# Cross attention: scores by quarters of the keys with VectorE's transposes, and the query folding in pieces

## The chip, the cores and the metric

The kernel runs on one core of a Trainium2 chip. The core has five engines with queues of their own: TensorE (PE in the profile; its weight loads are PEld), VectorE (DVE), ScalarE (ACT), GpSimd (POOL) and SyncE (SP). They share the on-chip memory SBUF. TensorE writes to PSUM, eight banks of 2 KB in each of 128 partitions, and VectorE and ScalarE read it. The metric is the device time of one execution in microseconds.

## The reference, cut to what matters

The network has four layers of cross attention, token mixing and a feed-forward part, twelve blocks in all. `x` is 16 batches of 64 tokens by 256, `ctx` 16 batches of 1024 keys by 192, all in float32. The change touches the cross attention of the first three layers:

```python
x = x + L0_xattn(layernorm(x), ctx, Wq, Wk, Wv, Wo)
...
x = x + L1_xattn(layernorm(x), ctx, Wq, Wk, Wv, Wo, bo)
...
x = x + L2_xattn(layernorm(x), ctx, Wq, Wk, Wv, Wo, bo)

def xattn(q_tokens, kv_tokens, Wq, Wk, Wv, Wo):   # per batch and head
    q, k, v = q_tokens @ Wq, kv_tokens @ Wk, kv_tokens @ Wv
    attn = softmax(q @ k.T * scale)
    return concat_heads(attn @ v) @ Wo            # + bo in L1 and L2
```

L0 has 16 heads of 16, L1 and L2 have 8 heads of 64.

## The kernel before, in words

The three blocks are two functions: `xattn_direct` for L0 and `xattn_folded` for L1 and L2. Both write their instructions in an order by hand: `set_order(True)` chains what goes to PE (`mm`, `tr`, lines 188 and 191), and the queues `dve` and `act` (line 72) do the same for VectorE and ScalarE. So each of these engines works strictly in the order of the program text, and an instruction that waits holds up all behind it. GpSimd's instructions are not chained by hand; they follow the program's order. Waits between engines come from the tiles that instructions read and write. A tile pool with `bufs=n` gives n buffers in turn, and the next user of a buffer waits for the last reader.

**`xattn_direct`.** 64 steps, for 16 batches b and 4 groups c of four heads. `qb` holds the scaled queries, for each group with the rows of the two heads of a pair masked (`own`), so that one matmul gives scores of two heads. A step works one ahead:

- `scores(b, c)` of the next step: four matmuls, each with 32 rows of keys, 128 query columns and 512 keys, into two `pss` tiles of 1024 columns (pool `ps_s`, two buffers of two banks);
- `least`: VectorE's negated maximum over the 1024 keys of each tile;
- `transposes`: the last step's probabilities `pr` are turned in eight 128x128 blocks by PE into a `pst` bank and copied to `pT` by ScalarE and VectorE, half of them early in the step, half late;
- `exps`: ScalarE's exponential with its sum `sm`, one instruction a tile; `shares`: VectorE divides by the sum;
- `project(b + 1, c)`: a quarter of the next batch's keys and values into two `psp` banks, copied to `kT` or `v` by VectorE and ScalarE;
- `values`: 32 matmuls of `v` with `pT` into `o`, one half of the bank `both` for even and one for odd batches; `keep` copies it out once a batch, and `output(t)` multiplies by `Wo` and adds to the residual `X`.

`queries` makes `qb`: the two instructions that mask it read the same bank `psq`, one on VectorE and one on ScalarE.

**`xattn_folded`.** Queries are multiplied by the key weights first (`queries`, then `fold`, for each of four head pairs m into `qw`), so that scores are taken against the raw context. `folded(g)` does all four m for four batches, and runs whole at the start and before batches 4, 8 and 12. There are 32 steps, for batch b and half h of the heads, again with scores one step ahead:

- `scores`: `qw` against `cT`, by quarters `qa` of the keys (32 output partitions each), into four `pss` banks of a pool of five. The tensors are so laid out that the 32 queries of a quarter lie beside the keys, and `turn` can transpose `pr` in 32x32 blocks on VectorE (`dve.transpose`, STREAM_TRANSPOSE) instead of on PE;
- `least`: maxima of each bank, then minima over the four partition quarters by small VectorE instructions (`nw`, `nmm`); `exps`: eight exponentials of 256 columns; `sums`: a matmul with `same` adds the sums of the quarters; `shares` divides, half on ScalarE, half on VectorE;
- `values(b - 1, h)` and, where h is 1, `others(b - 1)` and `keep(b - 1)`: the context weighed by the probabilities;
- `output(g2)`, every fourth batch in the step with h = 0: multiply by `Wv` per head (`oc` to `oT`), then by `Wo`, and add to `X`.

The layer norm in front of it, `norm_T`, handles all eight token tiles before the first fold. In L1 the steps 3 to 11 also issue `conv_taps`, and 14 to 29 `tap_rows`, for the next block.

Of the kernel before, what the change touches and what calls it, by code (L numbers as in the profile page):

```python
# [15 lines left out]
P = 128  # L16
# [62 lines left out]
class Net:  # L79
# [200 lines left out]
    def xattn_direct(self, L):  # L280
# [7 lines left out]

        nc, tc, a = self.nc, self.tc, self.a
# [6 lines left out]
        with ExitStack() as es:  # L296
# [3 lines left out]
            ps_s = es.enter_context(tc.tile_pool(name=f"{L}ps_s", bufs=2, space=PSUM))  # L300
# [7 lines left out]
            nc.vector.tensor_scalar(own, own, 0.25, None, ALU.mult)  # L308
            vs = [one.tile([P, NKC, H, 32], F32, name=f"v{i}") for i in range(2)]
# [43 lines left out]
            ctxs, kTs, os_ = {}, {}, {}  # L353
            both = ps_o.tile([P, 2, 4, TQ], F32, name="o")

            def project(b, piece):
# [6 lines left out]
                if piece < 2:  # L363
# [11 lines left out]
                    for i, copy in enumerate((dve.tensor_copy, act.copy)):  # L375
                        copy(kTs[b][:, 2 * piece + i, :], ps[i])
                else:
# [17 lines left out]
                    for n, copy in enumerate((dve.tensor_copy, act.copy)):  # L395
                        j = 4 * n + 2 * jh
                        copy(v[:, j : j + 2, :, :16], ps[n].rearrange("p (i h d) -> p i h d", i=2, d=16))

            def scores(b, c):
                pss = [ps_s.tile([P, S], F32, tag="s", name="pss") for _ in range(2)]  # L400
                for n in range(2):
                    for e in range(2):
                        r = (n ^ (c % 2)) * 64 + e * 32
                        ql = qb[r : r + 32, c, b].rearrange("p h q -> p (h q)")
                        self.mm(pss[e][:, n * 512 : (n + 1) * 512], ql, kTs[b][r : r + 32, c, :])
                return pss

            def least(ps):
                nm = self.small.tile([P, 1], F32, tag="nm", name="nm", bufs=4)
                dve.tensor_reduce(nm, ps, AX.X, ALU.max, negate=True)  # L410
                return nm

            def exps(ps, nm):
                pr = thr.tile([P, S], F32, tag="pr", name="pr", bufs=4)
                sm = self.small.tile([P, 1], F32, tag="sm", name="sm", bufs=4)
                act.activation(pr, ps, AF.Exp, bias=nm, accum_out=sm)
                return pr, sm

            def shares(pr, sm):
                dve.reciprocal(sm, sm)  # L420
                dve.tensor_scalar(pr, pr, sm, None, ALU.mult)

            def transposes(dst, pr, jh, copy):
                pt = ps_t.tile([P, 512], F32, tag="t", name="pst")
                for j in range(4):
                    jj = jh * 4 + j
                    self.tr(pt[:, j * P : (j + 1) * P], pr[:, jj * P : (jj + 1) * P])
                copy(dst[:, jh * 4 : jh * 4 + 4, :], pt.rearrange("p (j q) -> p j q", q=P))

            def values(b, c, pT):  # L430
                o = both[:, b % 2]
                for j in range(NKC):
                    for h in range(4):
                        self.mm(
                            o[32 * h : 32 * h + 32, c, :],
                            vs[b % 2][:, j, 4 * c + h, :],
                            pT[:, j, h // 2, (h % 2) * TQ : (h % 2 + 1) * TQ],
                            j == 0,
                            j == NKC - 1,
                        )  # L440

            def keep(b):
                if b % 2 == 0:
                    os_[b // 2] = two.tile([P, 4, 2, TQ], F32, tag="oT", name="oT")
                act.copy(os_[b // 2][:, :, b % 2, :], both[:, b % 2])
# [14 lines left out]
            project(0, 0)  # L460
            project(0, 1)
# [3 lines left out]
            pss = scores(0, 0)  # L465
            prs = [exps(pss[e], least(pss[e])) for e in range(2)]
            project(0, 2)
            project(0, 3)
            for p in prs:
                shares(*p)  # L470
            last = None
            for i, (b, c) in enumerate(steps):
                ahead = steps[i + 1] if i + 1 < len(steps) else None
                nxt, nms = [None, None], [None, None]
                if ahead:
                    pss = scores(*ahead)
                    nms = [least(ps) for ps in pss]
                pT = thr.tile([P, NKC, 2, P], F32, tag="pT", name="pT")
                transposes(pT[:, :, 0, :], prs[0][0], 0, act.copy)
                transposes(pT[:, :, 0, :], prs[0][0], 1, dve.tensor_copy)  # L480
                if ahead:
                    nxt = [exps(pss[e], nms[e]) for e in range(2)]
                    shares(*nxt[0])
                if b + 1 < B:
                    project(b + 1, c)
                if last:
                    values(*last)
                if ahead:
                    shares(*nxt[1])
                transposes(pT[:, :, 1, :], prs[1][0], 0, dve.tensor_copy)  # L490
                transposes(pT[:, :, 1, :], prs[1][0], 1, act.copy)
# [6 lines left out]
                if c == 0 and last:  # L498
                    keep(b - 1)
                if c == 1 and b % 2 == 0 and b > 0:  # L500
                    output(b // 2 - 1)
                prs, last = nxt, (b, c, pT)
            values(*last)
            keep(B - 1)
# [3 lines left out]
    def xattn_folded(self, L):  # L508
# [18 lines left out]
        with ExitStack() as es:  # L527
# [9 lines left out]
            self.norm_T(ps_s, "s")  # L537
# [2140 lines left out]
```

## Time and profile before

| | |
|---|---|
| median of 3 runs | 3169.97 us (3168.56 to 3195.57) |
| the profiled execution | 3170.8 us, of which its span is 3168.8 us |
| PE, DVE, ACT, POOL busy | 2940.9, 1960.3, 1348.4, 712.7 us |
| scores of L0, first and last start | 30.9 and 494.4 us |
| scores of L1 | from 766.8 us |
| scores of L2 | from 1659.2 us |

A row of the profile's groups names the source line, engine and operation, the tiles written and read (`pss<-kT,qb`), their shapes, how often, the busy time and the mean duration in ns; the idle time in front of it and what ended it stand last. In the order of time a row gives start and duration in us, and in brackets the idle time of the engine before it with what released it. Most PE and VectorE instructions of the ordered parts carry line 188, 191 or 72, those of the helpers, so they are told apart by their tiles. A float32 matmul is two MATMUL rows. PEclk is the clock that TensorE was granted, 1.00 at full speed. Matmul durations overlap, so starts are the better measure.

### The profile page before, as it was taken

The numbers are of one execution on the slowest core, as the hardware profiler recorded it, in microseconds if no ns is written. First come the engines' busy times: TensorE is split into PE (matmuls) and PEld (weight loads), VectorE is DVE, ScalarE is ACT, GpSimd is POOL, SyncE is SP. The second block draws the span as 40 slices with busy tenths as digits, with TensorE's granted clock in tenths as the row PEclk, the third lists the DMA queues.
The fourth block names the chain that finished last, engine by engine and source line by source line (L and its number), as shares of the span: only waits on it lengthen the run. The fifth ranks groups of instructions, "written<-read, shape, count | busy, mean of one in ns | idle before, by whom it ended". The sixth has DMA issues, their size and how long they took to land.

```text
span 3168.8 us, 64106 instructions
## 1 busy us (share of the span) xinstructions
PE 2940.9 (93%) x26912; PEld 1772.9 (56%) x26912; DVE 1960.3 (62%) x4061; ACT 1348.4 (43%) x3035; POOL 712.7 (22%) x784
## 2 busy tenths in 40 slices
PE   7999999898899999979978999997999899998797
PEld 4666666665445544458854545434665455556676
DVE  6888886524666665971127676757884676765611
ACT  3555554312554541013324454438861255654211
POOL 1000002411110001014411000024771355541131
PEclk9999999999999999978988999998999999999889
DMA  2000000013223313017851222201111211210233
GB/s 74 32 32 32 28 22 15 14 37 105 61 78 92 98 45 82 21 65 270 294 162 53 70 71 73 59 21 39 41 54 37 64 57 63 70 44 14 94 108 122
DMA packets 73793, 223.00 MB, mean 70 GB/s; under 512 B 17457, under 2 KB 28580, under 8 KB 66594
## 3 DMA queue, kind: packets, MB, share of 16 engines
q1 hardware_dynamic: 45936, 113.99, 11.9%
q0 software_dynamic: 21840, 99.39, 9.4%
q10 hardware_dynamic: 5730, 5.53, 0.6%
q8 instruction: 212, 3.47, 0.5%
q14 instruction: 75, 0.61, 0.1%
HBM read 210.00 MB, written 12.66 MB: 70 GB/s over the span
## 4 chain that ended last, share of the span: by engine, by line
PE 79%; DVE 9%; issue 4%; ACT 4%; POOL 3%; DMA 1%; SPq 0%; ACTq 0%; POOLq 0%; DVEq 0%
PE pss L188 13%; PE o L188 12%; PE pu L188 6%; PE psp L188 5%; PE pkv L188 5%; PE pd L188 5%; PE py L188 4%; PE pst L191 4%; PE psc L188 3%; PE po L188 2%; DVE nm L72 2%; ACT pr L72 2%; PE pb L191 2%; PE psi L188 1%; PE psq L188 1%
## 5 line engine op out<-in xcount | busy, mean ns | idle before, releaser
L188 PE MATMUL pss<-cT,qw 128*32 128x256 f32 x8192 | 371.5, 387 | 23.0 <-ACT pr L72 23.0
L72 DVE TENSOR_REDUCE nm<-pss 128x2 f32<-128x512 f32 (+1 forms) x384 | 309.3, 861 | 86.3 <-PE pss L188 86.3
L188 PE MATMUL o<-pT,cx 128*64 128x512 f32 (+1 forms) x1024 | 355.4, 607 | 0.0
L72 ACT ACTIVATE pr<-pss,nmm 128x256 f32<-128x256 f32 x512 | 234.3, 483 | 164.8 <-DVE nmm L72 164.8
L188 PEld LDWEIGHTS pss<-cT,qw 128*32 128x32 f32 x8192 | 205.0, 110 | 173.0 <-ACT pr L72 33.1
L188 PEld LDWEIGHTS o<-pT,cx 128*64 128x64 f32 (+1 forms) x1024 | 127.8, 165 | 200.2 <-issue 187.8
L205 POOL TENSOR_SCALAR rs<-mv 128x8 f32<-128x8 f32 (+3 forms) x52 | 10.0, 193 | 877.1 <-DVE mv L221 444.4
L188 PE MATMUL pkv<-wx,cT 128*128 128x512 f32 (+1 forms) x512 | 193.3, 632 | 0.6 <-issue 0.6
L72 ACT ACTIVATE pr<-pr,sm 128x256 f32<-128x256 f32 x256 | 109.1, 497 | 184.2 <-DVE sm L72 184.2
L72 DVE TENSOR_SCALAR pr<-pr,sm 128x256 f32<-128x256 f32 (+1 forms) x384 | 170.6, 486 | 6.6
L72 DVE TENSOR_TENSOR_SCAN h<-dA,pb 128x512 f32<-128x512 f32 x128 | 154.5, 1217 | 15.8 <-PE pb L191 9.4
L1444 POOL TENSOR_TENSOR h<-h,cb 128x1024 f32<-128x1024 f32 x64 | 151.4, 2368 | 53.3 <-DVE h L72 51.0
L2304 DVE TENSOR_SCALAR y<-pd,row 128x256 f32<-128x256 f32 x39 | 18.9, 484 | 225.1 <-PE pd L188 175.7
L72 DVE STREAM_TRANSPOSE pT<-pr 128x1024 f32<-128x1024 f32 x128 | 151.8, 1224 | 2.2
L188 PE MATMUL pd<-wd,hT 128*128 128x256 f32 x656 | 149.3, 382 | 3.0 <-DVE hT L2492 1.4
L72 ACT ACTIVATE pr<-pss,nm 128x1024 f32<-128x1024 f32 x128 | 142.5, 1113 | 11.4 <-DVE nm L72 8.8
L191 PE MATMUL pst<-ident,pr 128*128 128x128 f32 x1024 | 140.6, 280 | 5.8 <-DVE sm L72 1.9
L72 ACT COPY pT<-pst 128x512 f32<-128x512 f32 x128 | 74.9, 585 | 163.8 <-PE pst L191 163.8
L191 PEld LDWEIGHTS pst<-ident,pr 128*128 128x128 f32 x1024 | 109.4, 141 | 61.5 <-ACT pT L72 26.5
L188 PEld LDWEIGHTS pd<-wd,hT 128*128 128x128 f32 x656 | 123.1, 190 | 31.4 <-DVE hT L2492 6.2
L1618 POOL TENSOR_TENSOR rnk<-rnk,mhalf 128x8 f32<-128x8 f32 (+1 forms) x84 | 130.0, 1548 | 7.0
L188 PE MATMUL py<-h,ident 128*128 128x512 f32 x256 | 130.7, 596 | 0.0
(525 smaller groups left out, 5700.2 us busy)
## 6 DMA issues: line engine op xcount, KB each, us to landing
cT<-in_ctxT SPq DMA_DIRECT2D x32, 768.0 KB, 4.4
cx<-in_ctxP SPq DMA_DIRECT2D x32, 768.0 KB, 4.3
cT<-in_ctxT SPq DMA_DIRECT2D x32, 512.0 KB, 4.3
cT<-in_ctxT SPq DMA_DIRECT2D x64, 256.0 KB, 6.1
offb<-d_off SPq DMA_DIRECT2D x16, 576.0 KB, 3.6
cb<-d_C SPq DMA_DIRECT2D x16, 512.0 KB, 3.8
wu<-in_L_ffn_w POOLq DMA_DIRECT2D x8, 1024.0 KB
wd<-in_L_ffn_w POOLq DMA_DIRECT2D x8, 1024.0 KB
```

Source lines behind the costliest of these rows:

```text
L72: ins = getattr(self.engine, op)(*args, **kwargs)
L188: self.in_order(self.nc.tensor.matmul(out, lhsT=lhsT, rhs=rhs, start=start, stop=stop))
L191: self.in_order(self.nc.tensor.transpose(out, in_, self.ident))
L205: nc.gpsimd.tensor_scalar(t[:p, :n], in_, scale, eps, ALU.mult, ALU.add)
L1444: nc.gpsimd.tensor_tensor(hs[i], hs[i], cbs[hf, g], ALU.mult)
L1618: nc.gpsimd.tensor_tensor(r, r, self.mhalf[:, : n * H], ALU.pow)
L2304: nc.vector.tensor_scalar(y[:, i, :], po[:, i * D : (i + 1) * D], weight[:, g + i : g + i + 1], None, ALU.mult)
```

## The change

In `xattn_direct`, scores are taken for one half `hh` of a step at a time: 32 matmuls of 32 rows of keys by 32 query columns by 128 keys, by quarters `qa` of the keys. Both halves live in one tile `pss` of four banks with one buffer. `turn` on VectorE replaces `transposes` on PE. The maxima of the four quarters are gathered by four small GpSimd copies, reduced by VectorE, and spread by two more copies. Probabilities are no longer divided; the sums are added by PE once a batch (`sums`), spread over the partitions (`spread`) and multiplied into the values in `keep`. Both projection copies of a step go to ScalarE.

In `xattn_folded`, the norm works by halves of the tokens, `queries` and `fold` are issued one m at a time over the steps (`pieces`), `qw` is split in two tiles a group with three buffers, `output` is split into `heads` and `output(t)` in two steps, and the last batch's values are taken by halves of the columns.

```diff
-            ps_s = ... (name=f"{L}ps_s", bufs=2, space=PSUM)
+            ps_s = ... (name=f"{L}ps_s", bufs=1, space=PSUM)
...
+            pss = ps_s.tile([P, 2, 4, 2, P], F32, name="pss")
             both = ps_o.tile([P, 2, 4, TQ], F32, name="o")
...
+            def scores(b, c, hh):
+                kT = kTs[b][:, c].rearrange("p (k a y) -> p k a y", a=4, y=32)
+                for u in range(2):
+                    for qa in range(4):
+                        for n in range(2):
+                            for e in range(2):
+                                r = (n ^ (c % 2)) * 64 + e * 32
+                                self.mm(
+                                    pss[qa * 32 : (qa + 1) * 32, n, 2 * e + u, hh, :],
+                                    qb[r : r + 32, c, b, hh, u * 32 : (u + 1) * 32],
+                                    kT[r : r + 32, :, qa, :],
+                                )
+            def largest(hh):
+                nm = self.small.tile([P, 4], F32, tag="nm", name="nm", bufs=4)
+                dve.tensor_reduce(nm, pss[:, :, :, hh, :].rearrange("p n q k -> p q n k"), AX.XY, ALU.max, negate=True)
+                w = self.small.tile([32, 4, 4], F32, tag="nw", name="nw", bufs=4)
+                for qa in range(4):
+                    nc.gpsimd.tensor_copy(w[:, qa], nm[qa * 32 : (qa + 1) * 32])
+                return w
+            def least(w):
+                m = self.small.tile([P, 4], F32, tag="nmm", name="nmm", bufs=4)
+                dve.tensor_reduce(m[:32], w.rearrange("p a q -> p q a"), AX.X, ALU.min)
+                nc.gpsimd.tensor_copy(m[32:64], m[:32])
+                nc.gpsimd.tensor_copy(m[64:], m[:64])
+                return m
+            def exps(b, c, hh, m):
...
+                pr = thr.tile([P, 4, 2, P], F32, tag="pr", name="pr", bufs=3)
+                for q in range(4):
+                    act.activation(pr[:, q], pss[:, :, q, hh, :], AF.Exp, bias=m[:, q : q + 1],
+                        accum_out=sms[b][:, c, hh, q : q + 1])
+                return pr
+            def turn(b, c, hh, pr, lo=0, hi=4):
...
+                dve.transpose(
+                    pTs[b, c][:, :, hh, lo:hi].rearrange("p k q x -> p q k x"),
+                    pr[:, lo:hi].rearrange("p q n (k y) -> p q (n k) y", y=32),
+                )
+            def sums(b):
+                ps = both[:, 1].rearrange("p c q -> p (c q)")[:, :32]
+                for qa in range(4):
+                    self.mm(ps[qa * 32 : (qa + 1) * 32], same, sms[b].rearrange("p c h q -> p (c h q)"))
+                rc = two.tile([P, 32], F32, tag="rc", name="rc")
+                dve.reciprocal(rc, ps)
+                rds[b] = two.tile([P, 4, 2, 2, 2 * 32], F32, tag="rd", name="rd", bufs=1)
+                nc.gpsimd.tensor_tensor(
+                    rds[b].rearrange("p c h e (u x) -> p (c h e u) x", x=32), bc(rc, 2, 32), bc(same, 1, 32), ALU.mult
+                )
+            def spread(b):
+                for h in range(4):
+                    self.mm(both[32 * h : 32 * h + 32, 1], fourth, rds[b][:, :, h % 2, h // 2, :])
+                ra = two.tile([P, 4, TQ], F32, tag="ra", name="ra", bufs=1)
+                act.copy(ra, both[:, 1])
+                return ra
+            def keep(b, ra):
...
+                dve.tensor_tensor(os_[b // 2][:, :, b % 2, :], both[:, 0], ra, ALU.mult)
...
             for i, (b, c) in enumerate(steps):
                 ahead = steps[i + 1] if i + 1 < len(steps) else None
...
+                    scores(*ahead, 0)
+                    w = largest(0)
+                turn(b, c, 1, prs[1])
                 if ahead:
+                    prs[0] = exps(*ahead, 0, least(w))
                 if b + 1 < B:
+                    late = project(b + 1, c)
+                    act.copy(*late[0])
+                if ahead:
+                    scores(*ahead, 1)
+                    w = largest(1)
+                if c == 3:
+                    sums(b)
+                if c == 0 and last:
+                    ra = spread(b - 1)
                 if last:
                     values(*last)
                 if ahead:
+                    turn(*ahead, 0, prs[0], 0, 2)
+                    prs[1] = exps(*ahead, 1, least(w))
+                    turn(*ahead, 0, prs[0], 2, 4)
+                if c == 0 and last:
+                    keep(b - 1, ra)
+                if b + 1 < B:
+                    act.copy(*late[1])
```

In `xattn_folded`, cut to the order of the work:

```diff
-            self.norm_T(ps_s, "s")
...
             def queries(g, m):
-                ps = bank("psq")
+                ps = ps_t.tile([P, 512], F32, tag="t", name="psq")
...
             def fold(g, m):
-                if m == 0:
-                    qws[g] = two.tile([P, 2, G, H, TQ], F32, tag="qw", name="qw", bufs=1)
+                if m % 2 == 0:
+                    qws[g, m // 2] = two.tile([P, 2, G, 4, TQ], F32, tag="qw", name="qw", bufs=3)
-                pss = [bank("psqw") for _ in range(2)]
+                pss = [bank("psqw"), ps_t.tile([P, 512], F32, tag="t", name="psqw")]
...
-            folded(0)
+            norm(0)
+            normed(0)
+            for m in range(2):
+                queries(0, m)
+                fold(0, m)
             steps = [(b, h) for b in range(B) for h in range(2)]
             pss = scores(0, 0, None)
             now = exps(pss, least(pss))
+            for m in range(2, 4):
+                queries(0, m)
+                fold(0, m)
+            pieces = {8 * g + at: (g + 1, m) for g in range(B // G - 1) for m, at in enumerate((2, 4, 6, 7))}
+            pieces.update({0: (1, 0), 1: (1, 1)})
+            del pieces[2], pieces[4]
             for i, (b, h) in enumerate(steps):
-                if ahead and ahead[0] % G == 0 and ahead[1] == 0:
-                    folded(ahead[0] // G)
+                piece = pieces.get(i)
...
                 if ahead:
                     pss = scores(*ahead, lambda: sums(st, sm))
                 else:
+                    values(b - 1, range(4, NKC))
                     sums(st, sm)
                 dve.reciprocal(sm, st["sum"][:, :8])
                 shares(prs, sm, 1)
+                if piece:
+                    queries(*piece)
                 if ahead:
                     now = exps(pss, least(pss))
...
-                if b > 0:
-                    values(b - 1, h)
-                    if h == 1:
-                        others(b - 1)
-                        keep(b - 1)
+                if ahead and b > 0:
+                    values(b - 1, range(4 * h, 4 * h + 4))
+                if piece:
+                    fold(*piece)
+                if b > 0 and h == 1:
+                    others(b - 1)
+                    keep(b - 1)
+                if i == 1:
+                    norm(1)
+                if i == 2:
+                    normed(1)
...
-                if h == 0 and b % G2 == 1 and b > 1:
-                    output(b // G2 - 1)
+                if b % G2 == 1 and b > 1:
+                    if h == 0:
+                        heads(b // G2 - 1)
+                    else:
+                        for tt in range(T2 // P):
+                            output((b // G2 - 1) * T2 // P + tt)
...
-            for r in range(2):
-                values(B - 1, r)
-            others(B - 1)
+            for cols in (slice(0, 256), slice(256, 512)):
+                values(B - 1, range(NKC), cols)
+                others(B - 1, cols)
             keep(B - 1)
-            output(B // G2 - 1)
+            heads(B // G2 - 1)
+            for t in range(NT - T2 // P, NT):
+                output(t)
```

## The prediction

> **What bounds the kernel now.** I read the page, then busy time by stretches, then instructions in order of time in each stage that the change touches.
>
> ```profile
> PE 2940.9 (93%) x26912; PEld 1772.9 (56%) x26912; DVE 1960.3 (62%) x4061; ACT 1348.4 (43%) x3035; POOL 712.7 (22%) x784
> ```
>
> TensorE is the bound overall; whether it is in the touched stages shows in the stretches (the last three columns are granted clock, DMA share, GB/s):
>
> ```profile
> 31.00:477.00 446.00, 440.30 (x6208) 272.46 (x6208) 373.17 (x584) 251.37 (x438) 5.03 (x8) 1.00 0.09 30
> 778.00:799.00 21.00, 15.00 (x280) 8.06 (x274) 12.46 (x33) 11.09 (x42) 0.00 (x0) 0.83 0.22 52
> ```
>
> The first row is the steps of the first cross attention: PE busy 440.3 of 446 us, full clock. One of its 64 steps in order of time:
>
> ```profile
> 155.77 1.14 PE L188 MATMUL pss<-kT,qb 32*128 32x512 f32 x8
> 156.84 1.09 PE L191 MATMUL pst<-ident,pr 128*128 128x128 f32 x8
> 156.96 2.36 DVE L72 TENSOR_REDUCE nm<-pss 128x1 f32<-128x1024 f32 x2 [0.83 <-PE pss L188]
> 157.77 2.96 PE L188 MATMUL psp<-wv,cT 128*128 128x256 f32 x16
> 160.66 1.10 PE L188 MATMUL o<-pT,v 128*32 128x64 f32 x64
> 161.69 1.09 PE L191 MATMUL pst<-ident,pr 128*128 128x128 f32 x8
> 162.71 1.14 PE L188 MATMUL pss<-kT,qb 32*128 32x512 f32 x8
> ```
>
> PE starts: scores 1.07, transposes 0.93, projection 2.89, values 1.03, transposes 1.02: 6.94 us a step and no gap. With `output` and `queries`, which PE does between steps, the 63 steps from the first scores (30.9) to the last (494.4) take 463.5. VectorE works 6.2 us of it, ScalarE 4.6, hidden.
>
> **First cross attention, the good part.** Both sets of transposes leave PE: -1.95 us. Scores become 64 instructions a half, each 32 rows by 32 columns by 128 keys (a float32 matmul is two instructions). Nearest rows: `o` above, 64 instructions on four column tiles in 1.03 us, 16 ns each[...]; and, with eight tiles,
>
> ```profile
> 905.90 1.96 PE L188 MATMUL pss<-cT,qw 64*32 64x256 f32 x64
> 907.79 3.70 PE L188 MATMUL o<-pT,cx 128*128 128x512 f32 x8
> ```
>
> 64 in 1.88 us. The Trainium skill (TensorEngine Tiling (Array Packing), Theoretical Speedup) promises up to 16 times for 32x32 tiles. With 16 tiles and half the columns the 1.88 would be a quarter, 0.47 us. The 16 ns of `o` say 1.03, since each instruction has its weight load. Ends 0.47 and 1.88; I take 1.05, by `o`. PE then works 2 x 1.05 + 2.89 + 1.03 = 6.0 us a step, 0.9 less. VectorE loses the shares and pT copies and gains transposes at 1.2 us a half; ScalarE stays under 5 us. By busy time the step would be 6.0.
>
> **What it waits for.** `pss` is now one tile [P, 2, 4, 2, P] of four 2 KB banks, and the half `hh` is the second innermost axis: each bank holds keys of both halves. Both halves' scores, maxima and exponentials therefore use the same four banks. Two pairs of rows, each one DVE and one ACT instruction on disjoint interleaved outputs:
>
> ```profile
> 25.86 0.75 DVE L72 TENSOR_SCALAR qb<-psq,own 128x512 f32<-128x512 f32 x1 [1.19 <-PE psq L188]
> 26.64 0.69 ACT L72 ACTIVATE qb<-psq,own 128x512 f32<-128x512 f32 x1 [2.02 <-DVE qb L72]
> ...
> 761.80 0.69 DVE L72 COPY qw<-psqw 128x512 f32<-128x512 f32 x1 [3.58 <-PE psqw L188]
> 761.84 0.58 ACT L72 COPY qw<-psqw 128x512 f32<-128x512 f32 x1 [0.94 <-PE psqw L188]
> ```
>
> The `qw` pair reads two banks and runs side by side. The `qb` pair reads one bank and runs one after the other, 26.61 to 26.64, in all eight cases. Interleaved SBUF output isn't the reason (`qw` has it too); the shared bank is. That row shows two readers of the same columns. The rule of the skill (PSUM — Partial Sum Buffer, PSUM bank collisions raise a hardware error) goes further: any two of TensorE, VectorE and ScalarE must be kept apart per bank and quadrant, writes too, disjoint columns too. If only overlapping columns counted, half 1's scores could run under half 0's exponentials; by the rule they wait for the last of them. I take the rule, since the row has its sign.
>
> Then the program's order is one chain: scores 0, maxima 0, exponentials 0, scores 1, maxima 1, exponentials 1, next step. Its links, per half:
> - scores 1.05, hop 0.1 (hops of 0.03 to 0.1 are read between rows);
> - `largest`: 1024 elements from PSUM, 1.22 as `nm` now;
> - four GpSimd copies 32x4. No such row exists; nearest is
>
> ```profile
> L790 POOL COPY after<-gts 64x64 f32<-64x64 f32 x2 | 0.5, 234 | 0.0
> ```
>
> and TENSOR_SCALAR 128x4 at 192 ns. I take 0.18 each, with the hop 0.80; ends 0.1 each (a GpSimd memset of 32x1 is 91 ns) and 0.5 (moving between quadrants is unseen);
> - VectorE's 16-element minimum 0.19 and two hops 0.07, then two dependent GpSimd copies with hops 0.54;
> - four exponentials of 256 with accumulators. Existing ones
>
> ```profile
> L72 ACT ACTIVATE pr<-pss,nmm 128x256 f32<-128x256 f32 x512 | 234.3, 483 | 164.8 <-DVE nmm L72 164.8
> ```
>
> start 0.45 us apart, four take 1.92 to the last accumulator read; hops 0.13.
>
> Half 1 is 1.05 + 0.1 + 1.22 + 0.80 + 0.19 + 0.07 + 0.54 + 1.92 + 0.13 = 6.0. In half 0 the 1.2 us transpose of the previous half stands ahead of the minimum in VectorE's queue and outlasts the 0.80 of copies: 6.4. Step 12.4. The projection (2.9) lies beside half 0's chain, values (1.0) beside half 1's: hidden, so PE's savings buy nothing. Moving projection copies to ScalarE, `keep`, `output`, `queries`: in PE's or ScalarE's idle time, nothing.
>
> Two extras. `sums` puts on GpSimd, once a batch, a 1024-element product `rds`, between half 1's copies and its last two copies; its nearest row, a TENSOR_TENSOR 128x1024, is 2.37 us, about 2.1 of it in the chain: 16 x 2.1 = 34 us, 0.5 a step (ends 0 and 0.6). `rc`, `spread` and `ra` share the bank of `both` with values, which has slack. And PE idles some 2.4 us in half 0 and 3.9 in half 1. The second stretch above has idle gaps of 3.0 us every 10.4 us, and a mean clock of 0.83. For scores that follow them I add 0.5 a step (ends 0 and 1.5).
>
> Sum: 13.4 us a step, 63 steps: 844 against 463.5, **+381 us**. The ends of the unknown prices: all low, 11.1 us a step (+236); all high, about 17 (+608).
>
> **Second and third attention.** Steps there are PE-bound too: 9.15 and 12.74 us alternating, without gaps. Folding by pieces moves PE work of 2.1 us a piece and removes waits such as
>
> ```profile
> 859.81 2.08 PE L188 MATMUL psqw<-qT,wkT 64*128 64x256 f32 x8 [4.57 <-ACT qT L72]
> ...
> 1753.52 1.13 PE L188 MATMUL psqw<-qT,wkT 64*128 64x256 f32 x8 [1.65 <-ACT qT L72]
> ```
>
> - Three folds a layer, 8.5 us of PE work each: between the `pss` starts around them, less the 9.15 of the step, they take 15.5, 9.6, 9.6 in the second layer and 9.6, 11.3, 9.6 in the third. Waits saved: 9.2 and 5.0.
> - Two pieces go to steps 0 and 1, which wait for ScalarE anyhow: 2 x 2.1, less the 0.9 a step that the fifth bank now gives to `psqw`: 2.4 a layer.
> - `heads` and `output` in different steps: PE no longer waits for `oT`; 2 us in the second layer, 0 in the third (there 0.5 of wait stays).
> - Norm by halves starts the first fold some 7.8 us earlier, but pieces 2 and 3 stand behind the first eight exponentials on ScalarE, so the second scores come about 6.3 us later than now: gain 1.5 a layer. `norm(1)` is 2.3 us of VectorE in a step with 3 idle: nothing.
> - Last batch: four values matmuls fill the 3.5 us that PE waits for the last exponentials: 3.4 a layer. Halving columns changes no PE time.
> Together 9.2 + 5.0 + 4.8 + 2 + 3 + 6.8: -31 us (ends -45 and 0).
>
> **Total.** 3168.8 + 381 - 31 = 3519 of span, with 2.0 outside (3170.8 less 3168.8) 3521; the median of 3169.97 is the same within 1 us. I say **3521**.
>
> **Rivals.**
> - *The halves overlap (not slower).* Place: scores 1 against exponentials 0. It decides if banks don't tie them. Then the loop over two steps is scores 1.15, projection 2.89, scores 1.15, maxima 1.25, GpSimd 0.78, minimum 0.22, GpSimd 0.55, exponentials 1.9, transpose 1.25, minimum 0.25, GpSimd 0.55, exponentials 1.9: 13.84, or 6.92 a step, 436 against 463.5 if it also takes up `output` and `queries`. With half of the 34 us for `rds`: 3170.8 - 28 + 17 - 31 = 3129. For it: PE busy drops. Against: the `qb` pairs. Chance 0.06.
> - *GpSimd's copies between quadrants are dear*, 0.5 each: +1.9 in half 1, +1.5 in half 0, step 16.8, 3735. For it: no such copy in the trace. Against: small GpSimd rows of 0.1 to 0.25. Chance 0.10.
> - *The 32x32 tiles don't overlap* better than eight: scores 1.88, +1.7 a step, 3628. Against: `o` at 16 ns. Chance 0.10.
> - *Short chain*, scores 0.47, copies 0.1, no clock loss: 11.1 a step, 3376. Chance 0.10.
>
> **How the numbers follow.** The forecast itself has 0.64. The range 3360 to 3720 takes in the short chain, slow tiles and most of dear copies, and leaves out the overlap. One per cent (32 us) is about what a measurement tells from no change: slower 0.94 from all serial cases; the overlap's 3129 is 1.3% under 3171: of its 0.06, 0.04 faster and 0.02 same.
>
> **What would show it.** Right: in the first attention PE busy about half of each step, `pss` matmuls waiting for ACT `pr` twice a step, ACT `pr` of the first half ending before scores of the second start, about 12 to 14 us a step, clock under 1. In the second and third attention the waits for `qT` gone, steps as before. Wrong: `pss` of one half starting under exponentials of the other; a step near 7; or GpSimd copies beside 0.2 us by far. Scores of the first attention that span less than 650 us would prove the chain wrong.

## The result, and the profile after

The kernel after takes 3587.44 us (median of four runs, 3582.65 to 3588.34) against 3173.79 before: a ratio of 1.127, with an interval of 1.123 to 1.132. The change is slower by an eighth; the forecast was 3521. The profiled run took 3582.65 us, with a span of 3581.0, so 412.2 us are to be explained against the profile before.

First the page of the kernel after: busy time of the engines, the granted clock in 40 slices, and two groups of instructions (busy time and mean ns of one, then the idle time before them and what ended it).

```profile
PE 3032.8 (85%) x33888; PEld 1811.9 (51%) x33888; DVE 1913.4 (53%) x3970; ACT 1396.0 (39%) x3735; POOL 878.7 (25%) x1564
PEclk8787778776999999999779889999899899999979
L188 PE MATMUL pss<-kT,qb 32*32 32x128 f32 (+2 forms) x8576 | 200.4, 342 | 278.1 <-ACT pr L72 277.6
L434 POOL COPY nw<-nm 32x4 f32<-32x4 f32 x512 | 90.8, 177 | 614.0 <-DVE nm L72 598.4
```

PE's share fell from 93% to 85%. Its idle time (span less busy time) grew by 320 us, and most of that stands in front of one group: the scores of the first attention wait 278 us for ScalarE's exponentials. GpSimd's copies cost 177 ns each, so they are not dear in themselves. The clock is at six to eight tenths in the first ten slices, which are the first attention. Busy time in the stretch from the first scores to the last, before:

```profile
31.00:494.00 463.00, 457.27 (x6490) 284.02 (x6490) 388.79 (x607) 262.39 (x457) 10.35 (x13) 1.00 0.09 30
```

and after (span, then busy time of PE, PEld, DVE, ACT, POOL, then clock, DMA share, GB/s):

```profile
31.00:879.00 848.00, 534.90 (x13342) 309.73 (x13325) 344.73 (x519) 314.11 (x1159) 173.86 (x790) 0.79 0.05 17
```

No engine is busy for two thirds of it. One step in order of time shows why (some rows are left out, those of the weight loads among them):

```profile
301.73 1.07 PE L188 MATMUL pss<-kT,qb 32*32 32x128 f32 x64 [0.73 <-ACT pr L72]
302.91 1.23 DVE L72 TENSOR_REDUCE nm<-pss 128x4 f32<-128x1024 f32 x1 [3.75 <-PE pss L188]
304.20 0.83 POOL L434 COPY nw<-nm 32x4 f32<-32x4 f32 x4 [4.48 <-DVE nm L72]
304.46 1.10 PE L188 MATMUL o<-pT,v 128*32 128x64 f32 x64 [1.46 <-DVE rc L72]
305.11 1.91 POOL L486 TENSOR_TENSOR rd<-rc,same 128x1024 f32<-128x1024 f32 x1
305.62 0.71 DVE L72 STREAM_TRANSPOSE pT<-pr 128x512 f32<-128x512 f32 x1 [1.22 <-PE o L188]
306.26 0.13 DVE L72 TENSOR_REDUCE nmm<-nw 32x4 f32<-32x16 f32 x1
...
307.32 0.18 POOL L442 COPY nmm<-nmm 64x4 f32<-64x4 f32 x1
307.54 0.47 ACT L72 ACTIVATE pr<-pss,nmm 128x256 f32<-128x256 f32 x1 [5.38 <-POOL nmm L442]
...
308.90 0.48 ACT L72 ACTIVATE pr<-pss,nmm 128x256 f32<-128x256 f32 x1
...
309.52 1.52 PE L188 MATMUL pss<-kT,qb 32*32 32x128 f32 x64 [3.97 <-ACT pr L72]
...
316.15 0.58 PE L188 MATMUL pss<-kT,qb 32*32 32x128 f32 x33 [1.21 <-ACT pr L72]
```

Read the brackets from row to row: each engine is idle until the one before it in the chain has ended. Scores of half 1 (301.73), maximum, copies, minimum, copies, four exponentials, and only then the next scores (309.52), those of the next step's half 0; 6.6 us later half 1 again. This step takes 14.4 us, the mean is 13.49: it has the sums of a batch in it, so the minimum stands behind a transpose that waits for the values, these wait for `rc`, and `rd` on GpSimd holds the last copies back.

The same boundaries read in every trace give a table by stage, in us: the scores of the first attention from first to last (L0, in brackets for one of 63 steps), the stretch from the first product behind it (`pz`) to the end of the second attention (L1), the untouched `mamba_conv` (its first `psi` to its last `psT`), from there to the first `px` behind the third attention (L2; some 280 us of other blocks lie ahead of its first scores in this stretch, and some 220 us in that of L1), and the rest behind that. From e1_banks on, the kernels are the experiments.

| kernel | L0 scores | to the end of L1 | mamba_conv | L2 | rest | clock |
|---|---|---|---|---|---|---|
| before | 463.9 (7.36) | 664.9 | 165.8 | 739.9 | 1052.6 | 0.953 |
| after | 849.6 (13.49) | 665.4 | 177.8 | 748.7 | 1058.1 | 0.900 |
| e1_banks | 889.8 (14.12) | 665.5 | 177.9 | 747.3 | 1053.3 | 0.891 |
| e2_own_max | 603.8 (9.58) | 665.5 | 183.2 | 749.1 | 1053.5 | 0.930 |
| e3_direct_only | 845.6 (13.42) | 665.5 | 183.1 | 742.3 | 1053.4 | 0.903 |
| e4_folded_only | 465.6 (7.39) | 665.8 | 183.2 | 749.2 | 1053.0 | 0.946 |
| e5_whole_norm | 465.5 (7.39) | 656.8 | 178.0 | 734.5 | 1058.0 | 0.949 |
| e6_together | 464.0 (7.37) | 647.5 | 179.6 | 723.5 | 1059.8 | 0.951 |
| e8_two_tiles | 546.6 (8.68) | 665.8 | 169.2 | 747.0 | 1060.0 | 0.933 |
| e9_later | 545.5 (8.66) | 666.2 | 177.7 | 748.1 | 1060.6 | 0.930 |
| e10_both | 541.4 (8.59) | 647.5 | 179.6 | 721.6 | 1050.7 | 0.938 |
| e11_two_own | 489.2 (7.77) | 665.5 | 160.7 | 745.2 | 1065.7 | 0.945 |

After against before: +385.4 to the first `pz` (545.6 and 931.0), +0.5 in the stretch with L1, +12.0 in mamba_conv, +8.8 in L2, +5.5 in the rest; together the 412.2. The stretches with the second and third attention do not give back 31 us but cost 9, and an untouched stage takes 12.

During the experiments the kernel before ran at 3190 us rather than 3170 (medians 3190.5 to 3193.2 beside three groups of them), so ratios to it are used, and stages from the table.

### The profile page after: what moved, and what is told of

Read it like the earlier page. It is cut to its first block, busy times and chain, and to the rows that moved or that the text cites. A ratio compares the mean times of both kernels' runs of the same rounds, so it can differ in the third digit from the quotient of the medians.

```text
span 3581.0 us, 80085 instructions
## 1 busy us (share of the span) xinstructions
PE 3032.8 (85%) x33888; PEld 1811.9 (51%) x33888; DVE 1913.4 (53%) x3970; ACT 1396.0 (39%) x3735; POOL 878.7 (25%) x1564
## 3 DMA queue, kind: packets, MB, share of 16 engines
q1 hardware_dynamic: 45936, 113.99, 10.4%
## 4 chain that ended last, share of the span: by engine, by line
PE 56%; DVE 7%; issue 4%; ACT 3%; POOL 2%; DMA 1%; SPq 0%; POOLq 0%; ACTq 0%; DVEq 0%
PE pss L188 10%; PE o L188 8%; PE pu L188 5%; PE pkv L188 5%; PE pd L188 4%; PE py L188 4%; PE psc L188 3%; PE po L188 2%; ACT pr L72 2%; PE pb L191 2%; PE psi L188 1%; DVE nm L72 1%; PE pg L188 1%; PE psqw L188 1%; PE ptp L191 1%
## 5 line engine op out<-in xcount | busy, mean ns | idle before, releaser
L72 ACT ACTIVATE pr<-pss,nmm 128x256 f32<-128x256 f32 x1024 | 470.6, 478 | 648.4 <-POOL nmm L442 501.6
L188 PE MATMUL pss<-kT,qb 32*32 32x128 f32 (+2 forms) x8576 | 200.4, 342 | 278.1 <-ACT pr L72 277.6
L188 PE MATMUL o<-pT,cx 128*64 128x512 f32 (+3 forms) x1088 | 349.7, 574 | 2.4 <-issue 1.4
L72 DVE STREAM_TRANSPOSE pT<-pr 128x1024 f32<-128x1024 f32 (+1 forms) x319 | 319.2, 1018 | 42.0 <-PE o L188 37.9
L188 PEld LDWEIGHTS pss<-kT,qb 32*32 32x32 f32 (+1 forms) x8576 | 113.8, 117 | 364.8 <-ACT pr L72 334.1
L434 POOL COPY nw<-nm 32x4 f32<-32x4 f32 x512 | 90.8, 177 | 614.0 <-DVE nm L72 598.4
L188 PEld LDWEIGHTS o<-pT,cx 128*64 128x64 f32 (+1 forms) x1088 | 135.9, 163 | 183.2 <-issue 171.3
L72 ACT ACTIVATION_READ_ACCUMULATOR pr<-pss,nmm 128x1 f32 x1024 | 214.1, 209 | 0.0
L188 PE MATMUL psp<-wv,cT 64*128 64x256 f32 (+1 forms) x512 | 143.7, 511 | 3.8 <-DVE v L72 3.8
L188 PE MATMUL psp<-cT,wk 64*64 64x512 f32 (+1 forms) x512 | 137.7, 802 | 0.0
```

Source lines behind the costliest of these rows:

```text
L72: ins = getattr(self.engine, op)(*args, **kwargs)
L188: self.in_order(self.nc.tensor.matmul(out, lhsT=lhsT, rhs=rhs, start=start, stop=stop))
L434: nc.gpsimd.tensor_copy(w[:, qa], nm[qa * 32 : (qa + 1) * 32])
```

## The experiments

**Which part is it?** Two kernels take one half of the change each: `xattn_direct` of one kernel beside `xattn_folded` of the other.

> The first cross attention as after, the second and third as before. Theory (nearly all of the loss is the first): 385 us over before in that stage, and L1 and L2 give back the 9 us that they lost; what the untouched stages behind lost (12 us in mamba_conv, 6 further on, with TensorE at half clock for longer) stays if the first stage brought it: 3575 us. Rival (the slow clock behind comes from the second's and third's own change): 385 us alone, 3558 us. Second rival (the forecast of 31 us gained in the second and third holds and the trace of one execution deceives): 3610 us.

> The first cross attention as before, the second and third as after. Theory: the eight exponentials ahead of the folds of m = 2 and 3, and the norm of the second half of the tokens between steps 1 and 3, cost 17.3 us (L1) and 20.8 us (L2) and eat what the pieces and the halved last batch gain, so 9 us over before: 3178 to 3185 us. Rival one (the forecast): 31 us under before, 3140 us. Rival two (the untouched stages behind lose their 18 us here too, by the clock): 3197 us.

e3_direct_only took 3576.23 us, ratio 1.122 (1.118 to 1.126): the first attention carries the loss alone. Its 3576 is the theory's number, but counted from the 3191.59 us of before beside it the loss is 385 us, and that is the first rival's: the stages behind add nothing. e4_folded_only took 3196.8 us, ratio 1.002 (1.000 to 1.004), some 6 us over before. That excludes the forecast of 31 us under before, and also the 27 us over before of its second rival, whose 3197 was counted from 3170. mamba_conv took 183 us in both, in e4 with nothing changed ahead of L1; it took between 160.7 and 183.2 us in all runs, and the 160.7 stand in e11_two_own, which has the second and third attention of after. So nothing ties the 12 us there to the change. Its rows for before, after and e11_two_own show only the clock apart:

```profile
1210.00:1377.00 167.00, 165.77 (x849) 80.12 (x846) 144.27 (x270) 20.36 (x31) 16.82 (x28) 0.95 0.15 37
```

```profile
1596.00:1775.00 179.00, 177.75 (x849) 86.89 (x846) 144.16 (x270) 20.37 (x31) 16.87 (x28) 0.88 0.14 34
```

```profile
1234.00:1396.00 162.00, 160.75 (x848) 77.36 (x847) 140.15 (x266) 20.37 (x31) 16.88 (x28) 0.99 0.15 38
```

The same matmuls take 166, 178 and 161 us of PE at 0.95, 0.88 and 0.99 of the clock.

**What ties the halves? First, the banks.** The prediction held that the halves wait for each other because each has a part in all four banks of `pss`. The halves can be cut by pair of heads `e` instead; the array stays as it is, but a half is then two whole banks, the first and third or the second and fourth:

```diff
-  def scores(b, c, hh):  for u: for qa: for n: for e:
+  def scores(b, c, e):   for u: for hh: for qa: for n:
       mm(pss[qa*32:(qa+1)*32, n, 2*e+u, hh, :], ...)
-  largest: tensor_reduce(nm, pss[:, :, :, hh, :])
+  largest: tensor_reduce(nm, pss[:, :, 2*e:2*e+2])
-  turn:    one transpose of four blocks
+  turn:    two transposes of two blocks
```

> Only the first cross attention changes, against the kernel after. The two halves of a step are cut by pair of heads e instead of by parity hh: the same 32 products a half, the same exponentials, sums and transposes, but a half now lies in two banks of pss of its own, where both halves had a part in all four. Only two row tiles work at a time, so 64 instructions of scores may take up to 2 us where they took 1.0. Theory (the chain scores, maximum, exponentials runs once for each half one after the other because the halves share banks): with banks of their own the chain of one half lies beside the other's, the two waits of pss for the pr of ACT go, and a step falls from 13.5 us to what PE has to do, 6.5 to 8.5 us; 63 steps give 315 to 440 us, so about 3150 to 3275 us, with 3200 the likeliest. Rival (the small instructions between maximum and exponentials, the in-order queues of DVE and ACT or the two buffers of pT set the step, whatever the banks): a step stays above 12 us, at most 95 us are gained, 3490 us or more, and pss waits for ACT as before.

3607.2 us, ratio 1.131 (1.125 to 1.136): nothing gained, and a step of 14.12 us is even a little longer. The waits between 100 and 800 us (engine, line, what for: us in total, times, longest) and two rows in order of time:

```profile
PE pss L188 <- ACT pr L72: 203.6, 88, 4.0
```

```profile
303.13 0.48 ACT L72 ACTIVATE pr<-pss,nmm 128x256 f32<-128x256 f32 x1
...
303.75 1.63 PE L188 MATMUL pss<-kT,qb 32*32 32x128 f32 x64 [2.06 <-ACT pr L72]
```

The scores of one half still start just behind the last exponential of the other, which now reads different banks. The kernel after has 219.8 us of this wait in the same stretch. Banks of their own, inside one tile, are not enough.

**Second, the tile.** The waits between engines come from the tiles, and both halves are parts of one tile. So the same halves, in two tiles:

```diff
-  pss = tile([P, 2, 4, 2, P])                  # four banks
+  psh = [tile([P, 2, 2, 2, P]) for e in 0, 1]  # two banks each
```

> As e1_banks, with the halves e of pss in two tiles of two banks each instead of parts of one tile of four. In e1_banks the first scores of a half still waited for the exponentials of the other half, which read other banks; both are parts of one tile, so the suspicion is that the waits are set for the tile pss as a whole. Theory (the one tile chains the halves): the wait of the second scores for the exponentials of the first goes, a step falls from 13.5 us to what VectorE needs (5.6 us and its waits) or PE (6 to 8 us), 6.5 to 8.5 us, 3150 to 3275 us. Rival (the latency of maximum, copies, minimum and exponentials through in-order queues sets the step): above 12 us a step, 3490 us or more.

3270.5 us, ratio 1.028 (1.024 to 1.032), some 320 us less than after by the ratios; the step fell from 13.49 to 8.68 us, just over the range given. The wait is gone, between 100 and 500 us:

```profile
PE pss L188 <- ACT pr L72: 7.8, 12, 1.0
```

and scores of the second half run ahead of the first half's exponentials:

```profile
303.51 0.83 POOL L435 COPY nw<-nm 32x4 f32<-32x4 f32 x4 [1.83 <-DVE nm L72]
...
305.10 1.15 PE L188 MATMUL pss<-kT,qb 32*32 32x128 f32 x64
...
305.29 0.47 ACT L72 ACTIVATE pr<-pss,nmm 128x256 f32<-128x256 f32 x1 [1.18 <-POOL nmm L443]
```

At 303.51 the maximum of half 0 is on its way through GpSimd; at 305.10 PE writes half 1; at 305.29 ScalarE begins to read half 0. Against e1_banks the work is the same; the tiles differ, and with them the place of the banks, since the two of a half now lie side by side and no longer alternate with those of the other. So the chain needs no shared bank, and tiles of their own end it. That also excludes the rival of both runs, that maximum, copies and exponentials in their queues set the step in any case, though its numbers fitted e1_banks. Not tried were two halves of one tile in adjacent banks each, which would tell the tile from the range of banks that a half spans, and two tiles in shared banks. The half uses two of the array's row tiles instead of four, and 64 instructions take 1.15 us against 1.07: half as many array tiles cost little here.

**What do the small instructions cost?** Two kernels leave out the four copies, the minimum and the two copies back, one from after, one from e8_two_tiles:

```diff
-  w = ...; four gpsimd.tensor_copy(w[:, qa], nm[quarter qa])
-  tensor_reduce(m[:32], w, min); gpsimd.tensor_copy twice
+  m = nm
```

> The kernel after, in which each quarter of the keys keeps its own maximum in the first cross attention: the four copies of GpSimd to 32 rows, the minimum over quarters on VectorE and the two copies back are left out, so the quarters are not on one scale and the output isn't the reference's. All else stays, the shared banks too. Theory (the hops stand in the chain of each half): 0.80 + 0.26 + 0.54 us and the hops between them go from each half, 1.6 to 1.9 us, so 3.2 to 3.8 us of a step and 200 to 240 us in 63 steps: 3350 to 3390 us. In the half whose transpose outlasts the copies of GpSimd less may go, 1.2 us, which gives 3410 us at the upper end. Rival (they lie beside the transposes and the projection): under 60 us are gained.

> e8_two_tiles, in which each quarter of the keys keeps its own maximum in the first cross attention, so the quarters are not on one scale and the output isn't the reference's. In e2_own_max the same leaving out was worth 265 us, in a chain of two halves one after the other. Theory (the hops cost only where they stand in the chain of both halves): under two tiles they lie beside PE's work, at most 50 us go, 3220 us or more. Rival (the copies, or the queues that they hold, bound the step in any case): 150 us or more go, below 3120 us.

e2_own_max: 3322.02 us, ratio 1.042 (1.035 to 1.049). The step fell by 3.9 us, 246 us over 63 steps, somewhat more than the expected 240: the hops stand in the chain in full. e11_two_own: 3220.61 us, ratio 1.011 (1.006 to 1.016). The same seven instructions a half are worth 0.9 us a step, 57 us over the steps, once the halves overlap. The same instructions have two prices, a factor of four apart, and what runs beside them sets which.

**Is PE the bound of what is left?** In e8_two_tiles PE waited for `rc` and `ra` in every batch. Placing `sums` behind the last transposes and exponentials, and `spread` behind the values, takes both waits away:

```diff
-  if c == 3: sums(b)
-  if c == 0 and last: ra = spread(b - 1)
   if last: values(*last)
   turn(...); exps(...); turn(...)
-  if c == 0 and last: keep(b - 1, ra)
+  if c == 3: sums(b)
+  if c == 0 and last: keep(b - 1, spread(b - 1))
```

> As e8_two_tiles, with the sums of a batch issued behind the exponentials on VectorE, and the spreading of the reciprocals behind the values on PE, so that the values no longer stand behind a reciprocal of VectorE or the copy of ra on ACT. In e8_two_tiles PE waited 17.9 us for rc and 12.9 us for ra between 100 and 500 us. Theory (PE is what is left of the bound once the chain is cut): these 31 us in 400 go, some 40 us over the whole stage, 3230 us. Rival (VectorE or the chain of a half through its tile bounds the step): less than 15 us.

3276.96 us, ratio 1.026 (1.022 to 1.031), and 8.66 us a step: nothing. From 31 to 515 us, e8_two_tiles waited 20.8 us for `rc`, 15.2 for `ra` and 9.5 for `pr`. Here the first two are gone, and in their place stands

```profile
PE pss L188 <- ACT pr L72: 37.6, 22, 3.0
```

The waits put down to issue in front of `pss` grew from 7.1 to 15.2 us as well. So 36 us of stalls were removed and 36 came forward: PE waits until ScalarE has freed the tile of the half. The chain of one half through its own tile is late next, not PE's work; e11_two_own, where that chain is shorter and the step falls from 8.68 to 7.77 us, agrees.

**Why did the second and third attention not gain?** Before, the second scores of L1 start 10.83 us after the first:

```profile
766.81 6.55 PE L188 MATMUL pss<-cT,qw 128*32 128x256 f32 x144
777.64 4.48 PE L188 MATMUL pss<-cT,qw 128*32 128x256 f32 x48 [4.28 <-ACT pr L72]
```

In the kernel after, the same start in order of time:

```profile
1149.43 5.55 PE L188 MATMUL pss<-cT,qw 128*32 128x256 f32 x128
1154.91 1.13 PE L188 MATMUL psq<-xnT,wq 128*128 128x256 f32 x4
...
1162.35 0.51 ACT L72 ACTIVATE pr<-pss,nmm 128x256 f32<-128x256 f32 x1
...
1162.80 0.42 ACT L72 ACTIVATE qT<-psq 128x256 f32<-128x256 f32 x1
1163.28 2.08 PE L188 MATMUL psqw<-qT,wkT 64*128 64x256 f32 x8 [7.23 <-ACT qT L72]
...
1166.06 2.07 PE L188 MATMUL psq<-xnT,wq 128*128 128x256 f32 x4 [0.71 <-ACT qw L72]
...
1168.67 2.08 PE L188 MATMUL psqw<-qT,wkT 64*128 64x256 f32 x8 [0.53 <-ACT qT L72]
1170.67 1.93 PE L188 MATMUL pss<-cT,qw 128*32 128x256 f32 x16
```

The queries of m = 2 are ready at 1156, but `qT` stands behind the eight exponentials on ScalarE: PE idles 7.23 us, and then the two folds go one engine at a time. The second scores come 21.24 us after the first. And `norm(1)` with `normed(1)` comes between steps 1 and 3:

```profile
1204.93 0.80 PE L191 MATMUL psT<-ident,xn 128*128 128x128 f32 x2 [4.46 <-DVE xn L72]
```

PE's transposes stand behind VectorE's four `xn`, and the next scores stand behind PE's transposes: that step takes 16.86 us, before 9.94. Two kernels with the first attention of before undo this; the late folds and the late norm are undone together, so what each costs is read from the steps and not from a run of its own:

```diff
 e5_whole_norm
-  norm(0); normed(0); folds m = 0, 1 | scores(0, 0) | folds m = 2, 3
-  i == 1: norm(1)    i == 2: normed(1)
+  norm of all; folds m = 0 to 3 | scores(0, 0)
-  pieces of group 1 at 0, 1, 6, 7
+  pieces of group 1 at 2, 4, 6, 7
 e6_together, besides
-  h == 0: heads    h == 1: the output rows
+  h == 0: heads and the output rows
-  first piece of a group with the heads (2), then 4, 6, 7
+  first piece two steps ahead (0), then 4, 6, 7
```

> The first cross attention as before; the second and third as after, but with the norm of all tokens and all four folds of group 0 ahead of the first scores, as before. The folding by pieces for later groups, the heads and output rows in two steps and the halved last batch stay. Theory (the late folds and the late norm eat the gain): step 1 falls from 21 to 23 us to 11, step 4 from 17 to 19 us to 10, the start of the first scores moves back by 3 to 8 us; 11 to 14 us less than e4_folded_only in each of L1 and L2, about 25 us in all and 20 us under before. Rival (the pieces cost what the bursts did): the same as e4_folded_only, within 8 us.

> As e5_whole_norm, with the output rows of four batches in the step of their heads again, and the first piece of a group moved from the step of the heads two steps ahead. Theory: each heads and output pair of L2 loses 1.5 us and a piece beside the heads costs 1.9 us instead of 3.6: 4 us less in L2 for the rows, 3 times 1.7 us less in each of L1 and L2 at most: 4 to 14 us under e5_whole_norm. Rival (the PE work only moves): no difference above 3 us.

e5_whole_norm: 3168.98 us, ratio 0.994 (0.992 to 0.996), 20 us under before; e6_together: 3152.83 us, ratio 0.988 (0.985 to 0.992), 37 under. In the table the first took 9.0 us from the L1 stretch and 14.7 from L2 against e4_folded_only, and the second another 9.3 and 11.0. The 24 us of the first step are the 25 expected. Of the 20 of the second, 14 lie behind the first scores (4.8 in L1, from 431.1 to 426.3 us up to the first `psi`, and 9.0 in L2, from 449.5 to 440.5 up to the first `px`), the upper end of its 4 to 14. The rest lies ahead of them, where the two programs are the same: in e5_whole_norm the last product of the block ahead of L1 (`pd`) came 4.4 us later. The start of e6_together has no wait for `qT` above half a microsecond:

```profile
783.27 1.13 PE L188 MATMUL psq<-xnT,wq 128*128 128x256 f32 x4
784.87 1.13 PE L188 MATMUL psqw<-qT,wkT 64*128 64x256 f32 x8 [0.47 <-ACT qT L72]
787.28 5.35 PE L188 MATMUL pss<-cT,qw 128*32 128x256 f32 x64 [1.27 <-ACT pr L72]
```

**Both repaired halves together.** The first attention of e9_later with the rest of e6_together:

> The first cross attention of e9_later with the second and third of e6_together. Theory: the second and third give the 37 us under before that e6_together measured, the first lies at 7.3 to 7.8 us a step against 6.94 before, 20 to 55 us over before in that stage: 3150 to 3210 us, between e6_together and before. Rival (the first has come under 6.94 us a step): under 3150 us, faster than e6_together.

3225.16 us, ratio 1.012 (1.009 to 1.016): above the 3210 expected, in part since before ran 20 us slower here and in part since the first attention stays at 8.59 us a step. The fastest kernel is e6_together, which keeps the old first attention; it is 1.2% faster than before.

## Why the prediction was right, and where it wasn't

**First attention: right in size and in kind, with a cause that does not carry over.** 13.4 us a step were forecast; from half 0 to half 0 it is 13.36 in the mean (13.49 in the table, whose stretch also holds the last half 1); +381 us were forecast, and it is +385. The terms hold: scores 1.07 for the 1.05 (1.52 where the clock was lower), the maximum 1.23 for 1.22, four GpSimd copies 0.83 for the 0.80 with the hop. In the median, half 0 takes 6.63 us where 6.4 were said, and half 1 takes 6.05 for 6.0. In the fourth step of a batch half 1 is 1.7 us longer, by `rds`, where 2.1 were said. In the first it is 0.6 longer, where `spread` and `ra` were put at nothing. The two waits for exponentials a step and the clock under 1 are there as listed; PE is busy for 63% (535 of 848) where about half was said.

What the runs do not bear out is the reason for the chain. The prediction weighed the rule on PSUM bank collisions against the `qb` rows and took the shared bank as the tie. e1_banks gave the halves their own banks and kept the chain; e8_two_tiles gave them their own tiles and cut it. The `qb` pair could not tell the two apart: its two readers share a bank, but also the tile `psq`, where the two of `qw` have tiles of their own. In the kernel after, tile and bank tie the same halves, so either reason gives the same 3521, and to that extent the number was luck: for e1_banks the same reason gave 3200 us, and 3607 was measured. On its other question, whether only overlapping columns count, the forecast holds here, by bank or by tile: `values` writes one half of the columns of `both` and `rc` reads the other, and the row at 304.46 waits 1.46 us for `rc`. The rule is not refuted, since no run here lets two engines meet in one bank.

**Rivals.** Dear copies: excluded by 177 ns. Tiles that don't overlap: excluded by 1.07 us. The short chain had scores of 0.47, copies at 0.1 and no loss of clock; none of them is so. The overlap of the halves came to pass only in e8_two_tiles, at 8.68 us a step, where the rival's loop gave 6.92 with full clock and without `output` and `queries`. Even then the new form is slower than the old, at 7.36. Two sums of the ranges were off and decide nothing: with every price at its end a step comes to 10.6 or 19.6 us, not 11.1 or 17. And in the step shown before, VectorE and ScalarE are busy 5.96 and 4.09 us, not 6.2 and 4.6.

**What PE saved** was put at 0.9 us a step. From 31 to 570 us of e8_two_tiles:

```profile
31.00:570.00 539.00, 461.74 (x13189) 293.81 (x13195) 343.92 (x576) 307.30 (x1142) 171.75 (x780) 0.91 0.09 27
```

PE is busy 461.74 us, against 457.27 before at full clock. At 0.97, in e11_two_own, it is 432.52. So 25 us less of PE are seen there, where 0.9 us a step would be 57, and the lower clock in e8_two_tiles eats them.

**Second and third attention: the failed part.** -31 was forecast, +9 came. Three steps failed.
- *Pieces 2 and 3 behind the first exponentials.* The second scores were put 6.3 us later; they came 10.4 later in L1 and 12.1 in L2 (22.96 for 10.83). The working counted the wait for the exponentials but not the row of psq, qT, psqw, qw behind it, which goes through ScalarE one at a time, with PE's products slower than ahead of the wait (2.08 us for 1.13). The start before it gained 2.8 and 3.4 us, not 7.8.
- *`norm(1)` at nothing.* It cost 6.9 us in L1 and 8.7 in L2 (18.64 for 9.97). VectorE's idle time was taken as cover; what counted was PE's queue, in which the transposes wait for `xn` and the scores for the transposes.
- *`heads` and `output` in two steps at -2 and 0.* In L1 the pair of steps takes 29.91 us without a piece, before 29.92; in L2 31.38, so 1.5 us worse. And a piece in the step of the heads costs 3.6 us instead of 1.9.

What was right: the folds' waits went, since step 8 of L1 fell from 24.63 to 12.03 us and the bursts of 18.8 became steps of 11.1, with three more pieces of 1.9 to 3.6 us elsewhere, and the end of the last batch gained 4.8 and 3.2 us where 3.4 each was said. e6_together, without the failed steps, is 37 us faster than before: the sum was the right size for what the pieces can bring, and the order around them took it away.

**The total.** 3521 against the profiled 3582.65: of the 62 us, 4 lie in the first attention, 40 in the second and third, and 18 in the untouched stages, where the runs differ by as much among themselves.

## What to carry to other kernels

Before a tile is halved to let two stages overlap, check that the halves are separate tiles: here parts of one tile were chained though no byte and no bank was shared, and the chain's small links then cost their full latency (3.9 us a step here, 0.9 once the halves overlap). When work is moved later, list what stands ahead of it in every queue that it needs, and what stands behind it on PE: in this kernel the step with a norm that was priced at nothing, since VectorE was idle, became 7 to 9 us longer. When a removed stall buys nothing, look for the one behind it, as in e9_later.

## What the hardware showed unexpectedly

- **The clock falls where PE is idle.** In the first attention, PE's busy share and the granted clock fall together: 457 of 463 us at 1.00 (before), 432.5 of 479 at 0.97 (e11_two_own), 461.7 of 539 at 0.91 (e8_two_tiles), 535 of 848 at 0.79 (after). The chain seems charged twice: for the gap, and for the slower matmuls behind it (scores 1.07 or 1.52 us, the projection 2.96 or 3.97). The Trainium skill (TensorE: Matmul & The Clock Gate, HAM oscillation) states that waits longer than its window send PE back to half rate; here most scores behind a gap of 3.4 to 4 us took 1.5 us and those behind a short one 1.07, though one burst behind 3.95 us (at 230.08) took 1.07 too. No run varied the gap alone.
- **An untouched stage moved by 22 us.** mamba_conv took 160.7 to 183.2 us with the same instructions, with a clock of 0.99 to 0.85 where it was read (0.85 for 183.2 us, in e4_folded_only), and with PE busy 99% of it each time, so gaps are not all that lowers the clock. A difference of that size in one profile says nothing about an edit elsewhere.
- **Twice the array tiles hardly made the scores faster.** 64 instructions of 32x32 by 128 columns took 1.07 us with sixteen tiles and 1.15 with eight: 17 and 18 ns each.
